# Queries projected once, convolution output in image order, and later places for layer 1's and layer 3's small steps

## The chip, the cores and the metric

The kernel runs on one core of a Trainium2 chip. Time is device time in microseconds (us), the median of the runs: 2678.51 us before the change (three runs, 2678.45 to 2680.86). TensorE (PE in the profile) multiplies matrices into PSUM; VectorE (DVE) and ScalarE (ACT) work element by element; GpSimd (POOL) and SyncE (SP) mostly start transfers.

## The reference

A batch of 4 images of 64 x 64 pixels and 64 channels, in float32, goes through four layers:

- layer 0: self-attention over the 4096 pixels of an image. With q, k, v of 64 channels, `energy = q @ k.T`, softmax over its last axis, and `out[n] = sum_m attn[m, n] * v[m]`; then `gamma * out + x`.
- layer 1: a convolution block. Layer norm over channels, a pointwise product to 256 channels, a depthwise 3 x 3 convolution, the product of the two halves of channels, a channel gate (`sca`: the mean over pixels through a 128 x 128 matrix), a pointwise product back to 64 channels, and a residual. Then a second layer norm, a pointwise product to 256 channels, the product of halves, a product back to 64, and a residual.
- layer 2: attention over "channels by height" as the reference's reshape has it: scores are `xf.T @ xf` with 4096 x 4096 entries, softmax, products, residual.
- layer 3: a non-local block with 32 inner channels (`theta`, `phi`, `g`), softmax over 4096 x 4096, a product back to 64 channels, batch norm over all images, and a residual.

So each image has three 4096 x 4096 score matrices, whose exponentials are never stored as a whole.

## The kernel before

**Layout.** `X` holds an image as 128 partitions by 2048: 64 channels for each of two halves `s` of the pixels. `tok(x, s, j)` is the piece of 512 pixels number `j` of half `s`. Scores, exponentials and products are cut into items: an item of layer 0 makes 16 score matmuls into four PSUM tiles of 1024 columns, ScalarE takes the exponentials, and 8 product matmuls of an earlier item accumulate in PSUM. An item of layer 2 is 16 scores and 16 products, an item of layer 3 is 8 and 4. The matmuls use TensorE as several small arrays: 64 x 64 for the scores of layers 0 and 2, 128 rows by 64 columns for layer 0's products, 32 x 64 and 128 x 32 in layer 3.

**PSUM and buffers.** `new_ps` rotates through three PSUM tiles of 1024 columns, for scores and everything else; `new_acc` through two of 512 columns, for the accumulated products and for the sums `z` of layer 3. `new_t` rotates through two scratch tiles of 1024 columns, `new_e` through six tiles of exponentials.

**The order of the work** on TensorE, ScalarE and VectorE is written out by hand; each of these engines works through its list in that order. The main list has the items of all layers. The other steps (projections, layer 1, transposes) are generators in two lanes, `conv` and `misc`. Each item has a nominal time (3.6 us in layer 0, 4.6 in layer 2, 1.0 in layer 3), which is added to the lanes' clock twice per item, once after the scores and once after the products. A lane's step is recorded when the clock has reached its due time, and the number that a step yields is added to that due time:

```python
self.next = max(self.next, self.now - 8.0) + next(self.gens[0])   # Lane.step
while self.gens and self.next <= self.now: self.step()            # Lane.tick
```

So a yield says how much nominal time lies between two steps. A step with a small yield can be recorded in the same half item as the one before it.

**Steps that the change and the prediction touch.**

- `project0` (L961) makes layer 0's queries and values of the next image during the items of the present one. The folded weight `wq` has the same 64 columns twice, so each of four matmul groups (L971) writes the same queries to partitions 0 to 63 and 64 to 127 of `m.q`; L975 adds the bias and L983 that of the values.
- `norm` (L1052): squares on ScalarE (L1056), column sums on TensorE (L1062), then square, difference, Ln and Exp on 512 columns (L1067 to L1070), eight transfers that spread the result over the partitions (L1074), and two products on VectorE (L1082).
- `layer1`: pointwise products (L1091) into the padded image `pad` (L1113), nine taps per quarter and half of the channels on VectorE (L1128, L1130), the gate (L1133), the channel gate (L1136 to L1143), `pw2` (L1148) and its sum (L1156). Taps and gate write `yg` in the order of image columns; the reading matmul L1148 picks alternate columns out of it. In the second part, L1166 and L1168 take the two pointwise halves, and L1172 multiplies their product `u`.
- `close2` (L1252) divides layer 2's products and adds the residual (L1259, L1261); `open3` (L1267) starts with layer 3's theta projection (L1278), which reads that sum.
- In layer 3, VectorE adds up the exponentials (L1346, L1348), `totals` closes the sums (L1362), copies `z` out of PSUM (L1370), inverts it by Ln and Exp on ScalarE (L1374, L1375) and VectorE steps (L1376 to L1378). For the last half of images 0 and 1 it stands directly before the first layer-2 products of another image, which take two accumulators.

Of the kernel before, what the change touches and what calls it, by code (L numbers as in the profile page):

```python
# [8 lines left out]
F32 = mybir.dt.float32  # L9
# [682 lines left out]
def fast_path(ctx: ExitStack, tc: tile.TileContext, a: dict, out: bass.AP, bad):  # L692
    nc = tc.nc
# [29 lines left out]
    def new_big(name):  # L723
        return big.tile([128, 4096], F32, tag="big", name=name)
# [236 lines left out]
    def project0(b):  # L961
        x, m = X[:, b], im[b]
        m.q, yv = new_big("q"), new_big("yv")
        m.y = yv[:, 0:2048]
        m.v = yv[:, 2048:4096].rearrange("p (t c) -> p t c", c=C)
        for j, w in ((0, "q"), (0, "v"), (1, "q"), (2, "q"), (1, "v"), (3, "q")):
            ps = new_ps()
            if w == "q":
                for o in range(0, 128, 64):
                    for s in range(2):  # L970
                        mm(  # L971
                            ps[o : o + 64, bass.ts(s, 512)], wq[64 * s : 64 * s + 64, o : o + 64],
                            tok(x, s, j), start=True, stop=True,
                        )
                nc.vector.tensor_scalar_add(  # L975
                    m.q[:, 0:N].rearrange("p (s n) -> p s n", s=2)[:, :, bass.ts(j, 512)],
                    ps.rearrange("p (s n) -> p s n", s=2), bqk,
                )
            else:
                for i in range(8):  # L980
                    mm(ps[:, bass.ts(i, 128)], x[:, bass.ts(8 * j + i, 128)], wv, start=True, stop=True)  # L981
                for s in range(2):
                    nc.vector.tensor_add(  # L983
                        m.v[:, 16 * s + 8 * j : 16 * s + 8 * j + 8, :],
                        ps.rearrange("p (t s c) -> p t s c", s=2, c=C)[:, :, s, :],
                        bv.unsqueeze(1).to_broadcast([128, 8, C]),
                    )
            yield 3.4
# [62 lines left out]
    def norm(x, y):  # L1051


        sq = [new_t("sq"), new_t("sq")]
        for i in range(2):
            act(sq[i], x[:, bass.ts(i, 1024)], AF.Square)  # L1056
        yield 4.0
        ps = new_ps()
        for i, src in enumerate(((x, x), (sq[0], sq[1]))):
            for j in range(4):  # L1060
                c = 512 * j if i == 0 else 512 * (j % 2)
                mm(  # L1062
                    ps[32 * j : 32 * j + 32, bass.ts(i, 512)], jsel, src[j // 2][:, c : c + 512],
                    start=True, stop=True,
                )
        t = new_t()
        act(t[:, 0:512], ps[:, 0:512], AF.Square)  # L1067
        stt(t[:, 0:512], t[:, 0:512], -1.0, ps[:, 512:1024], ALU.mult, ALU.add)
        act(t[:, 0:512], t[:, 0:512], AF.Ln, bias=eps1)
        act(t[:, 512:1024], t[:, 0:512], AF.Exp, scale=-0.5)  # L1070
        yield 7.0
        for j in range(4):
            for h in range(2):
                nc.sync.dma_start(  # L1074
                    out=y[64 * h : 64 * h + 64, bass.ts(j, 512)],
                    in_=t[32 * j + 16 * h : 32 * j + 16 * h + 16, 512:1024]
                    .unsqueeze(1).to_broadcast([16, 4, 512]),
                )
        yield 26.0
        for jp in range(2):  # L1080
            cols = bass.ts(jp, 1024)
            nc.vector.tensor_mul(y[:, cols], y[:, cols], x[:, cols])  # L1082
            yield 1.8

    def layer1(b):
# [10 lines left out]

        y = xn.tile([128, 2048], F32, tag="xn", name="xn")
        yield from norm(x, y)
        yg = new_big("yg")[:, 0:N].rearrange("p (w h) -> p w h", h=H)
        ysum = sm.tile([128, 4], F32, tag="ysum", name="ysum")  # L1100
        for r in (1, 0):
            pad = new_pad()
            nc.gpsimd.memset(pad[:, 0:PW], 0.0)
            nc.gpsimd.memset(pad[:, 65 * PW : 66 * PW + 2], 0.0)
            nc.gpsimd.memset(
                pad[:, PW : 65 * PW].rearrange("p (w h) -> p w h", h=PW)[:, :, 0:1], 0.0
            )
            inner = pad[:, PW + 1 : 65 * PW + 1].rearrange("c (p q s h) -> c q p s h", p=2, s=2, h=PW)
            for j in range(4):
                ps = new_ps()  # L1110
                pointwise(ps, pw1, r, y, j)
                for s in range(2):
                    act(  # L1113
                        inner[:, bass.ts(j, 4), :, s, 0:H],
                        ps[:, bass.ts(s, 512)].rearrange("c (q p h) -> c q p h", p=2, h=H),
                        AF.Identity, bias=pwb[:, 0, r : r + 1],
                    )
                yield 3.5
            for j in range(4):
                w0 = 16 * j  # L1120
                y2 = yg[:, w0 : w0 + 16, :]
                out_ = y2 if r else new_t("y1").rearrange("p (w h) -> p w h", h=H)
                for k in range(9):
                    o = (w0 + k % 3) * PW + k // 3
                    win = pad[:, o : o + 16 * PW].rearrange("p (w h) -> p w h", h=PW)[:, :, 0:H]
                    wt = V("L1_conv_dw_w", 2 * k + r)
                    if k == 0:
                        nc.vector.tensor_scalar(out_, win, wt, V("L1_conv_dw_b", r), ALU.mult, ALU.add)  # L1128
                    else:
                        stt(out_, win, wt, out_, ALU.mult, ALU.add)  # L1130
                    yield 1.8
                if not r:
                    stt(y2, out_, 1.0, y2, ALU.mult, ALU.mult, accum_out=ysum[:, j : j + 1])  # L1133
                    yield 1.8
        ytot = sm.tile([128, 1], F32, tag="ytot", name="ytot")
        nc.vector.tensor_reduce(ytot, ysum, AX.X, ALU.add)  # L1136
        yield 3.5
        ps = new_ps()
        mm(ps[:, 0:1], sca, ytot, start=True, stop=True)
        ch = sm.tile([128, 1], F32, tag="ch", name="ch")  # L1140
        nc.vector.tensor_scalar(ch, ps[:, 0:1], 1.0 / N, V("L1_conv_sca_b"), ALU.mult, ALU.add)
        pw2s = sm.tile([128, C], F32, tag="pw2s", name="pw2s", bufs=1)
        nc.vector.tensor_scalar_mul(pw2s, pw2, ch)  # L1143
        yield 3.5
        for j in range(4):
            ps = new_ps()
            for s in range(2):
                mm(  # L1148
                    ps[64 * s : 64 * s + 64, 0:512], pw2s,
                    yg.rearrange("c (p q s) h -> c q p s h", p=2, s=2)[:, bass.ts(j, 4), :, s, :],  # L1150
                    start=True, stop=True,
                )
            t = new_t()
            act(t[:, 0:512], ps[:, 0:512], AF.Identity, bias=resb[:, 0:1], scale=V("L1_conv_beta"))
            xs = x[:, bass.ts(j, 512)]
            nc.vector.tensor_add(xs, xs, t[:, 0:512])  # L1156
            yield 3.5
        z = xn.tile([128, 2048], F32, tag="xn", name="xn")
        yield from norm(x, z)
        for j in range(4):  # L1160
            t, u = new_t(), new_t("u")
            for r in range(2):
                ps = new_ps()
                pointwise(ps, pw3, r, z, j)
                if r == 0:
                    act(t, ps, AF.Identity, bias=pwb[:, 1, 0:1])  # L1166
                else:
                    stt(u, ps, pwb[:, 1, 1:2], t, ALU.add, ALU.mult)  # L1168
                yield 3.5
            ps = new_ps()  # L1170
            for s in range(2):
                mm(ps[64 * s : 64 * s + 64, 0:512], pw4, u[:, bass.ts(s, 512)], start=True, stop=True)  # L1172
            act(t[:, 0:512], ps[:, 0:512], AF.Identity, bias=resb[:, 1:2], scale=V("L1_conv_gamma"))
            xs = x[:, bass.ts(j, 512)]
            nc.vector.tensor_add(xs, xs, t[:, 0:512])
            yield 3.5
# [75 lines left out]
    def close2(b):  # L1252
        x, m = X[:, b], im[b]
        nc.vector.tensor_reduce(sums2[:, b, :], m.zs, AX.X, ALU.add)
        rz = sm.tile([128, 32], F32, tag="rz2", name="rz2")
        nc.vector.reciprocal(rz, sums2[:, b, :])
        for i in range(4):
            d = m.ph[:, bass.ts(i, 512)].rearrange("p (w h) -> p w h", h=H)
            nc.vector.tensor_mul(d, d, rz[:, bass.ts(i, 8)].unsqueeze(2).to_broadcast([128, 8, H]))  # L1259
            xs = x[:, bass.ts(i, 512)]  # L1260
            nc.vector.tensor_add(xs, xs, m.ph[:, bass.ts(i, 512)])  # L1261
            yield 2.0

# [46 lines left out]
    def layer3(b):  # L1312
# [53 lines left out]

        def totals(nb):
            sums()
            yz = st["yz"]
            nc.scalar.copy(yz[:, 512:1024], st["z"])  # L1370

            t = new_t("inv")
            r, d = t[:, 0:512], t[:, 512:1024]
            act(r, yz[:, 512:1024], AF.Ln)  # L1374
            act(r, r, AF.Exp, scale=-1.0)  # L1375
            nc.vector.tensor_mul(d, yz[:, 512:1024], r)  # L1376
            stt(d, d, -2.0, r, ALU.add, ALU.mult, accum_out=inv3[:, b, nb : nb + 1])
            stt(yz[:, 0:512], d, -1.0, yz[:, 0:512], ALU.mult, ALU.mult)  # L1378

# [224 lines left out]
```

## Time and profile before

| | us |
|---|---|
| span of the profiled execution | 2674.3 |
| TensorE busy | 2614.5 |
| ScalarE busy | 1722.9 |
| VectorE busy | 1349.0 |
| layer 0's scores and products (L1005, L1030) | 473.3 and 467.3 |
| layer 2's (L1208, L1225) | 472.4 and 467.9 |
| layer 3's (L1324, L1352) | 313.4 and 272.0 |
| queries (L971), all images | 17.0 |
| taps, other than first (L1130), both halves | 164.3 and 164.3 |

A group's line in the profile has the engine, the operation, the tiles it writes and reads, their shapes, the count, the busy time and the mean of one. A float32 matmul appears as two records, so x128 of L971 are 64 matmuls. A timeline row has start, duration, and in brackets the idle time of the engine just before it and what ended that. Layer 0 runs to about 1050 us with layer 1 beside it, layer 2 of images 0 and 1 to about 1580 with the rest of layer 1, and then layers 3 and 2 take turns.

### The profile page before, as it was taken

The page shows a single profiled execution, that of the slowest core. Times are in us where ns is not written, and L with a number is a line of the kernel's source. Part 1 is how long each engine was busy: PE and PEld are TensorE (multiplying, and loading weights), DVE is VectorE, ACT ScalarE, POOL GpSimd, SP SyncE. Part 2 cuts the span into 40 slices and gives each one's busy share as a digit, 9 for nine tenths or more (in the row PEclk, how much of TensorE's full clock was granted, in tenths as well). Part 3 has the DMA queues.
Part 4 walks back from the last instruction along what each step waited for, and adds up shares of the span by engine and source line. Part 5 has one row for each costly group of instructions (what it writes and reads, how often), then busy time and mean ns, then how long its engine had stood idle before and what let it go on. Part 6 is the DMA issues. An engine that isn't in the chain of part 4 may idle for free.

```text
span 2674.3 us, 50670 instructions
## 1 busy us (share of the span) xinstructions
PE 2614.5 (98%) x22393; PEld 831.3 (31%) x22393; DVE 1349.0 (50%) x1505; ACT 1722.9 (64%) x2796; POOL 16.4 (1%) x66
## 2 busy tenths in 40 slices
PE   8999999999999999999999999999999999999996
PEld 3333233323323333433333322243322333322222
DVE  3242387733777336641475148810068600098997
ACT  4545655555565665665656568856578756578886
POOL 2000000000000000000000000000000000000000
PEclk9999999999999999999999999999999999999998
DMA  3000000000000100010010100010000010010001
GB/s 73 1 1 1 16 1 1 1 17 17 1 1 1 33 16 1 1 32 1 17 33 1 33 1 1 2 33 1 17 2 1 5 29 1 1 33 1 1 2 65
DMA packets 22505, 33.30 MB, mean 12 GB/s; under 512 B 3484, under 2 KB 11909, under 8 KB 22277
## 3 DMA queue, kind: packets, MB, share of 16 engines
q1 hardware_dynamic: 21205, 28.87, 4.8%
q8 instruction: 177, 2.90, 0.5%
q0 software_dynamic: 672, 0.56, 0.1%
q10 hardware_dynamic: 400, 0.56, 0.1%
q14 instruction: 51, 0.42, 0.1%
HBM read 4.80 MB, written 4.19 MB: 3 GB/s over the span
## 4 chain that ended last, share of the span: by engine, by line
PE 92%; DVE 4%; ACT 2%; issue 1%; DMA 0%; ACTq 0%; DVEq 0%
PE acc L1030 17%; PE ps L1005 17%; PE acc L1225 16%; PE ps L1208 15%; PE ps L1324 10%; PE acc L1352 9%; PE ps L1091 2%; DVE yg L1130 1%; PE accz L1341 1%; DVE tg L1348 1%; ACT e L1216 1%; PE ps L981 1%; PE ps L1172 1%; PE ps L1148 1%; PE ps L1062 1%
## 5 line engine op out<-in xcount | busy, mean ns | idle before, releaser
L1010 ACT ACTIVATE e<-ps 128x1024 f32<-128x1024 f32 x512 | 516.6, 1024 | 336.4 <-PE ps L1005 217.7
L1216 ACT ACTIVATE e<-ps 128x1024 f32<-128x1024 f32 x512 | 516.6, 1024 | 317.4 <-PE ps L1208 317.2
L1330 ACT ACTIVATE e<-ps 128x1024 f32<-128x1024 f32 x512 | 495.4, 1022 | 87.3 <-PE ps L1324 78.9
L1348 DVE TENSOR_TENSOR tg<-tg,e 128x2048 f32<-128x2048 f32 x214 | 490.4, 2291 | 24.1 <-ACT e L1330 5.8
L1005 PE MATMUL ps<-X,q 64*64 64x512 f32 x4096 | 473.3, 596 | 8.4 <-ACT e L1010 4.4
L1208 PE MATMUL ps<-ko 64*64 64x512 f32 x4096 | 472.4, 593 | 5.4 <-ACT e L1216 2.4
L1225 PE MATMUL acc<-e,X 64*64 64x512 f32 x4096 | 467.9, 591 | 2.1 <-DVE X L1037 1.5
L1030 PE MATMUL acc<-e,vq 128*64 128x512 f32 x2048 | 467.3, 598 | 0.0
L1037 DVE SCALAR_TENSOR_TENSOR yv<-acc,gam,yv 128x512 f32<-128x512 f32 x224 | 168.0, 750 | 345.6 <-PE acc L1030 334.2
L1324 PE MATMUL ps<-tg,ph 32*64 32x512 f32 x4096 | 313.4, 613 | 0.5 <-ACT e L1330 0.5
L1352 PE MATMUL acc<-e,tg 128*32 128x512 f32 x2048 | 272.0, 603 | 1.5 <-ACT yz L1358 1.5
L1208 PEld LDWEIGHTS ps<-ko 64*64 64x64 f32 x4096 | 158.7, 133 | 291.6 <-issue 190.2
L1225 PEld LDWEIGHTS acc<-e,X 64*64 64x64 f32 x4096 | 164.1, 133 | 273.7 <-issue 255.3
L1005 PEld LDWEIGHTS ps<-X,q 64*64 64x64 f32 x4096 | 142.3, 132 | 322.7 <-issue 220.3
L1030 PEld LDWEIGHTS acc<-e,vq 128*64 128x64 f32 x2048 | 136.5, 136 | 315.8 <-issue 297.5
L1233 DVE TENSOR_TENSOR ph<-ph,acc 128x512 f32<-128x512 f32 x16 | 11.0, 687 | 383.4 <-ACT ph L1232 383.4
L1130 DVE SCALAR_TENSOR_TENSOR y<-pad,vec,y 128x1024 f32<-128x1024 f32 x128 | 164.3, 1284 | 6.3 <-ACT pad L1113 2.4
L1130 DVE SCALAR_TENSOR_TENSOR yg<-pad,vec,yg 128x1024 f32<-128x1024 f32 x128 | 164.3, 1283 | 3.7
L1324 PEld LDWEIGHTS ps<-tg,ph 32*64 32x64 f32 x4096 | 79.8, 129 | 221.2 <-issue 142.4
L1352 PEld LDWEIGHTS acc<-e,tg 128*32 128x32 f32 x2048 | 43.5, 108 | 202.3 <-issue 196.3
L1216 ACT ACTIVATION_READ_ACCUMULATOR e<-ps 128x1 f32 x512 | 106.3, 208 | 0.0
L1010 ACT ACTIVATION_READ_ACCUMULATOR e<-ps 128x1 f32 x512 | 106.2, 207 | 0.0
(179 smaller groups left out, 964.5 us busy)
## 6 DMA issues: line engine op xcount, KB each, us to landing
xn<-t SPq DMA_DIRECT2D x64, 128.0 KB
ph<-tg SPq DMA_DIRECT2D x64, 128.0 KB
ko<-ko SPq DMA_DIRECT2D x16, 256.0 KB
out_dram<-o SPq DMA_DIRECT2D x8, 512.0 KB
xr<-in_x_dram SPq DMA_DIRECT2D x14, 256.0 KB
xr<-in_x_dram ACTq DMA_DIRECT2D x2, 256.0 KB
pw<-in_L_conv_pw_w_dram POOLq DMA_DIRECT2D x4, 64.0 KB, 4.2
sca<-in_L_conv_sca_w_dram POOLq DMA_DIRECT2D x1, 64.0 KB, 5.7
```

Source lines behind the costliest of these rows:

```text
L1005: mm(ps[64 * c : 64 * c + 64, bass.ts(r, 512)], m.q[rows_, 128 * t + 64 * c : 128 * t + 64 * c + 64], x[rows_, bass.ts(g, 512)], start=Tru ...
L1010: act(es[g // 2][:, bass.ts(g % 2, 1024)], ps, AF.Exp, bias=SHIFT0, accum_out=zs[:, g : g + 1],)
L1030: mm(accs[g][64 * r : 64 * r + 64, :], vq, es[half][:, 1024 * g + 512 * r : 1024 * g + 512 * r + 512], start=t == 2 * p, stop=t == 2 * p + 1,)
L1037: stt((x if p == 15 else m.y)[:, cols], accs[g], gam0, (m.y if p else x)[:, cols], ALU.mult, ALU.add,)
L1130: stt(out_, win, wt, out_, ALU.mult, ALU.add)
L1208: mm(ps[64 * c : 64 * c + 64, bass.ts(r, 512)], m.ko[rows_, 128 * jb + 64 * c : 128 * jb + 64 * c + 64], m.ko[rows_, bass.ts(2 * ib + r, 5 ...
L1216: act(es[n, jb], ps, AF.Exp, bias=SHIFT2, accum_out=m.zs[:, jb, ib : ib + 1])
L1225: mm(acc[r][64 * c : 64 * c + 64, :], xw[rows_, jb, :], es[n, jb][rows_, bass.ts(c, 512)], start=jb == 0, stop=jb == 31,)
L1324: mm(tiles[kp][64 * c : 64 * c + 64, bass.ts(i, 512)], m.ph[rows_, 128 * mc + 64 * c : 128 * mc + 64 * c + 64], m.th[rows_, bass.ts(nb, 51 ...
L1330: act(e[:, bass.ts(kp, 1024)], tiles[kp], AF.Exp)
L1348: nc.vector.tensor_add(esum, esum, e)
L1352: mm(st["y"][32 * k : 32 * k + 32, :], m.gx[:, mc, :], e[:, bass.ts(k, 512)], start=mc == 0, stop=mc == 31,)
```

## The change

Five edits. For images 1 to 3, `project0` multiplies each half of the queries once, into the 64 partitions of one of its two places, and transfers bring them to the other 64; image 0 keeps the old way. The convolution writes `yg` in image order (the last tap of the first half of channels, and the gate, in two parts each), so that `pw2` reads it contiguously. Several yields in `norm` and `layer1` are moved or made larger, so that Ln and Exp, the channel gate and the last pointwise product are recorded later than what feeds them; the wait before the normalising products is made shorter. `close2` yields longer after its last sum, so that `open3` comes later. `totals` reads `z` from PSUM directly and no longer copies it.

```diff
-        for j, w in ((0, "q"), (0, "v"), (1, "q"), (2, "q"), (1, "v"), (3, "q")):
+        once = ((0, "once"), (0, "v"), (1, "once"), (1, "v"))
+        for j, w in once if b else ((0, "q"), (0, "v"), (1, "q"), (2, "q"), (1, "v"), (3, "q")):
             ps = new_ps()
-            if w == "q":
+            if w == "once":
+                for o in range(2):
+                    for s in range(2):
+                        mm(
+                            ps[64 * o : 64 * o + 64, bass.ts(s, 512)], wq[64 * s : 64 * s + 64, 0:64],
+                            tok(x, s, 2 * j + o), start=True, stop=True,
+                        )
+                qs = m.q.rearrange("p (s n) -> p s n", s=2)
+                for o in range(2):
+                    own, other = slice(64 * o, 64 * o + 64), slice(64 - 64 * o, 128 - 64 * o)
+                    n = bass.ts(2 * j + o, 512)
+                    nc.vector.tensor_scalar_add(
+                        qs[own, :, n], ps[own, :].rearrange("p (s n) -> p s n", s=2), bqk[own, :]
+                    )
+                    nc.sync.dma_start(out=qs[other, :, n], in_=qs[own, :, n])
+            elif w == "q":
...
         stt(t[:, 0:512], t[:, 0:512], -1.0, ps[:, 512:1024], ALU.mult, ALU.add)
+        yield 5.0
         act(t[:, 0:512], t[:, 0:512], AF.Ln, bias=eps1)
         act(t[:, 512:1024], t[:, 0:512], AF.Exp, scale=-0.5)
-        yield 7.0
+        yield 4.0
...
-        yield 26.0
+        yield 14.0
...
-        yg = new_big("yg")[:, 0:N].rearrange("p (w h) -> p w h", h=H)
-        ysum = sm.tile([128, 4], F32, tag="ysum", name="ysum")
+        yg = new_big("yg")
+        yw = yg.rearrange("c (s q p h) -> c p q s h", s=2, p=2, h=H)
+        ysum = sm.tile([128, 8], F32, tag="ysum", name="ysum")
...
+                    elif k < 8 or not r:
+                        stt(y1, win, wt, y1, ALU.mult, ALU.add)
                     else:
-                        stt(out_, win, wt, out_, ALU.mult, ALU.add)
+                        for s in range(2):
+                            stt(
+                                yw[:, j // 2, bass.ts(j % 2, 8), s, :], win[:, s:16:2, :], wt,
+                                y1[:, s:16:2, :], ALU.mult, ALU.add,
+                            )
                     yield 1.8
                 if not r:
-                    stt(y2, out_, 1.0, y2, ALU.mult, ALU.mult, accum_out=ysum[:, j : j + 1])
+                    for s in range(2):
+                        y2 = yw[:, j // 2, bass.ts(j % 2, 8), s, :]
+                        stt(
+                            y2, y1[:, s:16:2, :], 1.0, y2, ALU.mult, ALU.mult,
+                            accum_out=ysum[:, 2 * j + s : 2 * j + s + 1],
+                        )
...
         nc.vector.tensor_reduce(ytot, ysum, AX.X, ALU.add)
-        yield 3.5
+        yield 5.0
...
         nc.vector.tensor_scalar_mul(pw2s, pw2, ch)
-        yield 3.5
+        yield 5.0
...
-                    ps[64 * s : 64 * s + 64, 0:512], pw2s,
-                    yg.rearrange("c (p q s) h -> c q p s h", p=2, s=2)[:, bass.ts(j, 4), :, s, :],
+                    ps[64 * s : 64 * s + 64, 0:512], pw2s, yg[:, bass.ts(4 * s + j, 512)],
...
                     stt(u, ps, pwb[:, 1, 1:2], t, ALU.add, ALU.mult)
-                yield 3.5
+                yield 5.0 if r else 3.5
...
             nc.vector.tensor_add(xs, xs, m.ph[:, bass.ts(i, 512)])
-            yield 2.0
+            yield 2.0 if i < 3 else 6.0
...
-            yz = st["yz"]
-            nc.scalar.copy(yz[:, 512:1024], st["z"])
+            yz, z = st["yz"], st["z"]
...
-            act(r, yz[:, 512:1024], AF.Ln)
+            act(r, z, AF.Ln)
             act(r, r, AF.Exp, scale=-1.0)
-            nc.vector.tensor_mul(d, yz[:, 512:1024], r)
+            nc.vector.tensor_mul(d, z, r)
```

More of the change, by code (lines that the diff above doesn't have):

```diff
@@ L1120, in layer1 @@
                 w0 = 16 * j
-                y2 = yg[:, w0 : w0 + 16, :]
-                out_ = y2 if r else new_t("y1").rearrange("p (w h) -> p w h", h=H)
+                y1 = new_t("y1").rearrange("p (w h) -> p w h", h=H)
                 for k in range(9):
@@ L1127, in layer1 @@
                     if k == 0:
-                        nc.vector.tensor_scalar(out_, win, wt, V("L1_conv_dw_b", r), ALU.mult, ALU.add)
-                    else:
-                        stt(out_, win, wt, out_, ALU.mult, ALU.add)
+                        nc.vector.tensor_scalar(y1, win, wt, V("L1_conv_dw_b", r), ALU.mult, ALU.add)
+                    elif k < 8 or not r:
+                        stt(y1, win, wt, y1, ALU.mult, ALU.add)
+                    else:
+                        for s in range(2):
[3 more added lines that the diff above has]
+                            )
                     yield 1.8
                 if not r:
-                    stt(y2, out_, 1.0, y2, ALU.mult, ALU.mult, accum_out=ysum[:, j : j + 1])
+                    for s in range(2):
[4 more added lines that the diff above has]
+                        )
                     yield 1.8
```

## The prediction

> **What bounds the kernel now.** I read the page's busy shares and chain first, then TensorE's waits, then the timeline around each wait.
>
> ```profile
> PE 2614.5 (98%) x22393; PEld 831.3 (31%) x22393; DVE 1349.0 (50%) x1505; ACT 1722.9 (64%) x2796; POOL 16.4 (1%) x66
> ...
> PE 92%; DVE 4%; ACT 2%; issue 1%; DMA 0%; ACTq 0%; DVEq 0%
> ```
>
> TensorE is busy for 2614.5 of 2674.3 us and carries 92% of the chain. So two things shorten this kernel: fewer matmuls, and fewer of the 59.8 idle us. TensorE's timeline puts about 11 us of idle time in the first 15 us and about 21 after 2600 us; the change touches neither. Some 29 us lie between, and the waits name them:
>
> ```profile
> PE ps L1172 <- DVE u L1168: 5.0, 3, 1.8
> PE ps L1005 <- ACT e L1010: 4.4, 5, 1.2
> PE ps L1278 <- DVE X L1261: 4.1, 3, 2.8
> PE ps L1005 <- DVE q L975: 3.3, 4, 1.4
> PE ps L1208 <- ACT e L1216: 2.4, 2, 1.2
> ```
>
> Each is a matmul recorded too soon behind the ScalarE or VectorE work that feeds it or frees its PSUM tile. The columns are total, times, longest.
>
> **What the Trainium skill says.** "TensorEngine Tiling (Array Packing)", Key Properties: changing the tiling mode drains the array, tiles of one mode run in parallel. The trace agrees: 16 score matmuls (32 records) take 3.43 us where layer 2 uses 64x64 tiles throughout, and 3.59 in layer 0, which alternates with 128x64. "Perfetto Trace Analysis", Optimization Strategy: on the engine that matters, find the gaps and make what they wait for start sooner; that is how I count below. "VectorE: DVE Perf Modes", the TRN2 errata section: a fixed cost per instruction, so halves cost more than the whole. The trace agrees (692 ns for 512 elements, 1219 for 1024).
>
> **The change part by part.**
>
> *Queries once, images 1 to 3.* Four q groups of four matmuls become two, so six groups go in all. One inserted group moves the next start by 0.91 to 0.97 us (L971 at 395.95, next at 396.86; 653.30, next at 654.26). At 0.94: −5.6 us. VectorE's work stays: one 128-partition add of 1.28 us becomes two of 64 partitions; a 64-partition copy of the same 1024 elements takes 1.215 (L1190), so I take 1.28 each. The copies to the other 64 partitions are DMAs of 256 KB; they have over ten items of 7.2 us before layer 0 of that image reads them, so they cost nothing. But a query group's PSUM tile is now held for 2.56 us, and only three such tiles exist. The place to look is image 2, whose projection falls among layer 1's taps:
>
> ```profile
> 397.28 2.60 DVE L1130 SCALAR_TENSOR_TENSOR yg<-pad,vec,yg 128x1024 f32<-128x1024 f32 x2
> 399.80 1.28 DVE L975 TENSOR_SCALAR q<-ps,bqk 128x1024 f32<-128x1024 f32 x1
> ```
> ```profile
> 399.18 1.09 PE L1005 MATMUL ps<-X,q 64*64 64x512 f32 x8 [0.42 <-ACT e L1010]
> 401.13 1.09 PE L1005 MATMUL ps<-X,q 64*64 64x512 f32 x8 [0.86 <-DVE q L975]
> ```
>
> The add queues behind two taps, and scores wait for its tile: that item's 16 matmuls took 5.18 us (396.86 to 402.04) instead of 3.49, a later one 4.11: 2.3 us lost now. In the changed program's recorded order, VectorE has T4, two q adds, two v adds, the layer-0 pair, its scale, a tap and a split tap, then two q adds. From the same start (391.8): 2.56 + 1.4 gives 395.7, pair and scale 397.9, taps 2.7 give 400.6, adds end at 403.2; the third score tile wants that PSUM at 396.86 + 1.8 = 398.7. Loss 4.5. Image 1: the first v add ends at 5.3 us where its tile is wanted at 4.8: 0.6. Image 3, with pads beside it: 0.8 by the same count. Together +5.9 −2.3 = +3.6.
>
> *Ln and Exp later.* Now ScalarE does Square, waits for VectorE, then Ln and Exp, while four score exponentials stand behind:
>
> ```profile
> 287.11 0.60 ACT L1067 ACTIVATE t<-ps 128x512 f32<-128x512 f32 x1 [2.05 <-PE ps L1062]
> 288.52 0.72 ACT L1069 ACTIVATE t<-t,eps 128x512 f32<-128x512 f32 x1 [0.81 <-DVE t L1068]
> 289.28 0.63 ACT L1070 ACTIVATE t<-t 128x512 f32<-128x512 f32 x1
> 289.81 1.00 ACT L1010 ACTIVATE e<-ps 128x1024 f32<-128x1024 f32 x1
> ```
> ```profile
> 290.96 1.09 PE L1005 MATMUL ps<-X,q 64*64 64x512 f32 x8 [1.24 <-ACT e L1010]
> ```
>
> The fourth tile of scores waits 1.24 us. The same gap of 1.18 stands at 539.5, 883.4, 1194.5 and 1273.9: 6.0 us. A lane steps at most once per 3.6 (layer 0) or 4.6 (layer 2) nominal us, so a yield of 5.0 always puts half an item, 3.4 us or more of TensorE, in between. In the new order every Ln has exponentials or such a half item ahead of it. −6.0. The DMA behind Exp lands within 8 us of it (Exp ended near 1272.8, second product at 1280.8); the first product now comes 18 nominal us after Exp, so the shorter yield costs nothing.
>
> *Pointwise products and the sca steps later*, by the same 5.0: the three waits of L1172 (1.58, 1.84, 1.55), L1139 (0.98), L1148 (0.69): −6.6. *Projections later* (6.0 after the last sum): 2.79 + 0.98 + 0.28: −4.0.
>
> *A side effect of moved steps.* In image 2's second norm the new order records the squares and their sums in one step, right behind 16 scores. ScalarE ends its exponentials some 1.6 us after those scores, then two squares of 1.07: the second half of the sums can start 3.7 us after the scores instead of 0.9: +2.8. ScalarE has nothing urgent behind it. Elsewhere the squares keep a half item of room. Layer 2's transposes (waits of 0.66, 0.42, 0.87, 0.47 now) get new neighbours: −1.0, with 0 to −1.5 as bounds.
>
> *Image order.* Eight taps or gates per image become two of half size: 0.16 us more each for a tap (2 x 0.72 against 1.284), 0.24 for a gate with its accumulator: 1.6 us of VectorE per image. Beside layer 0, nine taps and their share of layer-0 work take 15.73 us in 16.16, ten steps with a gate 17.55 in 17.95; with the additions 15.9 and 17.8. It fits, barely, so 0. TensorE's pw2 matmuls read contiguously instead of in runs of 64; L1148 costs 16.8 us as L1172 costs 17.1 with contiguous reads, so nothing is gained.
>
> *No copy of z.* ScalarE saves 0.60 seven times. Inside layer 3 it is nearly full, and after each of five totals the scores stretch (2.07 against 1.11 us); they shorten by the copy: −3.1. At the two turns from layer 3 to layer 2 the copy was what freed the accumulator:
>
> ```profile
> 1728.33 0.60 ACT L1358 COPY yz<-acc 128x512 f32<-128x512 f32 x1
> 1728.79 0.62 ACT L1370 COPY yz<-accz 128x512 f32<-128x512 f32 x1
> 1729.45 0.63 ACT L1374 ACTIVATE inv<-yz 128x512 f32<-128x512 f32 x1
> 1730.11 0.63 ACT L1375 ACTIVATE inv<-inv 128x512 f32<-128x512 f32 x1
> ```
>
> The new products need z's buffer; the old copy released it at 1729.4. Now the VectorE product after Exp releases it: 1728.8 + 0.63 + 0.66 + 0.7 = 1730.9, 1.45 later; behind that matmul stand all of TensorE's scores. Twice: +2.9.
>
> Sum: −5.6 + 3.6 − 6.0 − 6.6 − 4.0 + 2.8 − 1.0 − 3.1 + 2.9 = −17.0. From 2678.5: **2661.5 us**.
>
> **The rivals.** *No new waits*: VectorE runs ahead more than counted, and the 5.9, 2.8 and 2.9 do not appear: 2678.5 − 28.6 = 2650. For it: most VectorE idle time lies just before those points. Against: the query wait is there already, with half the hold time. *New waits take half*: all three query projections lose 4.5 as image 2 does (+7.6), and another sum or transpose loses 2: 2671. For it: three PSUM tiles are few wherever lanes meet. Against: images 1 and 3 project without taps beside them. *VectorE becomes the bound beside layer 0*: if half a tap with strided rows costs as much as a whole one, eight times 1.28 us per image meet a slack of 0.4: 0.88 x 8 x 3 = 21 us: 2682, slower than before. For it: VectorE is 93% busy there already. Against: 512-element rows of every kind take 0.69 to 0.75.
>
> **How the numbers follow.** The counted sum 0.60; no new waits 0.15; half 0.18; VectorE bound 0.07. The range of 2652 to 2671 covers the counted case with its unknowns (transposes 1.5, query waits ±4, totals ±3) and most of the two neighbours. Faster by over 0.2% means under 2673.2: 0.60 + 0.15 + 0.12 = 0.87; within 0.2%: 0.07; slower 0.06.
>
> **What would show it.** TensorE's waits on u, on Exp-delayed e, on ytot and on the last sum of close2 gone; a wait of some 4 us on the query add near 390 to 410 us; one wait of 2 to 3 us of the sums of squares on sq in layer 2; products of layer 2 waiting over 1 us on VectorE's inv twice; scores after totals at 1.45 us rather than 2.07. I am wrong if VectorE's layer-0 pair makes TensorE's L1030 matmuls wait during taps, or if the query copies' DMAs are waited for.

## The result and the profile after

The changed kernel takes 2656.11 us (median of four, 2655.98 to 2657.46) against 2679.69 of the kernel before beside it: a ratio of 0.9912, 95% interval 0.9895 to 0.9929. That is 23.6 us less, where 17.0 were predicted; 2656.1 lies inside the range of 2652 to 2671, 5.4 us under the forecast.

The same two lines of the page, the busy shares and the chain:

```profile
PE 2606.3 (98%) x22345; PEld 824.7 (31%) x22345; DVE 1352.9 (51%) x1553; ACT 1718.8 (65%) x2789; POOL 16.4 (1%) x66
...
PE 94%; DVE 3%; ACT 2%; issue 1%; DMA 0%; ACTq 0%; DVEq 0%
```

TensorE has 48 fewer records and 8.2 us less work, VectorE 48 more instructions and 3.9 us more, ScalarE 7 fewer and 4.1 us less (seven copies of z at 0.60). TensorE's share of the chain rises from 92% to 94%: waits went.

TensorE's waits in the same view (total, times, longest), leaving out the start and the end, which hardly changed:

```profile
PE ps L1021 <- DVE q L980: 4.1, 2, 3.1
...
PE acc L1252 <- DVE inv L1402: 1.6, 2, 0.8
PE ps L1078 <- ACT sq L1072: 1.6, 1, 1.6
PE ps L1235 <- ACT ko L1217: 1.6, 3, 0.7
```

Of the five waits shown of the kernel before, only that on the query add is still high in the list, and it has grown. The waits on u, on ytot and on layer 2's last sum (X) are gone, of those of scores on e two of 0.4 us are left in layers 0 and 2. What stands there now are the three waits that the prediction named: the query add, the squares, and VectorE's inv at the turns.

Idle time isn't all that a wait costs, so below I also use the *shift*: the start of each group of score or product matmuls in one trace, less the start of the same group in another. It is flat while both kernels do the same, and steps where one loses time. Taken from 62.6 us (after the constants are set up) to the last group of layer 3, the kernel before is 23.2 us behind the changed one, like the timed 23.6. The spans of the two pages differ by only 20.0, because from 47 to 54 us the changed kernel's trace has a stretch in which TensorE was granted half its clock, 3.1 us of start that the other trace doesn't have.

| stretch of the changed kernel | counted in the prediction | shift |
|---|---|---|
| 63 to 276 us: image 1's queries | −1.3 | −1.2 |
| 276 to 789: two norms, two query projections, sca of image 0 | −3.9 | −4.5 |
| 789 to 1044: one norm, transposes | −1.5 | −0.6 |
| 1044 to 1552: layer 2 of images 0 and 1 | −9.3 | −15.3 |
| 1552 to 2563: layer 3, two turns, last projection | −1.2 | −1.6 |

The transposes' −1.0 is divided by their waits. So the surplus of 6 us lies in one stretch, layer 2 of images 0 and 1 with layer 1 of images 2 and 3 beside it.

**The new waits, one by one.** First TensorE, then VectorE, in the timeline of the changed kernel, where image 2's queries are projected (start, duration, instruction, idle time before it):

```profile
403.63 1.09 PE L1021 MATMUL ps<-X,q 64*64 64x512 f32 x8 [3.14 <-DVE q L980]
```
```profile
399.65 1.41 DVE L1150 SCALAR_TENSOR_TENSOR yg<-pad,vec,y 128x512 f32<-128x512 f32 x2
400.98 2.59 DVE L980 TENSOR_SCALAR q<-ps,bqk 64x1024 f32<-64x1024 f32 x2
```

The two adds queue behind a tap and a split tap and end at 403.57; the scores start at 403.63. Those sixteen score matmuls took 7.46 us (397.08 to 404.54) in place of 3.49: 3.97 lost, 4.5 predicted. Image 1 waits 0.2, image 3 1.0. A half tap takes 0.75 us (counted 0.72), an add of 64 partitions 1.28 (counted 1.28).

ScalarE in the first norm of layer 1, where the Ln stood ahead of four score exponentials:

```profile
289.92 1.02 ACT L1026 ACTIVATE e<-ps 128x1024 f32<-128x1024 f32 x1 [0.36 <-PE ps L1021]
...
293.92 0.74 ACT L1086 ACTIVATE t<-t,eps 128x512 f32<-128x512 f32 x1
```

Now four exponentials run first, and TensorE's 32 score records go through in 3.67 us with no gap.

The sums of squares in image 2's second norm, TensorE's timeline:

```profile
1154.86 1.06 PE L1078 MATMUL ps<-X,jsel 128*32 128x512 f32 x8
1157.54 2.00 PE L1078 MATMUL ps<-sq,jsel 128*32 128x512 f32 x8 [1.62 <-ACT sq L1072]
1159.47 1.95 PE L1252 MATMUL acc<-e,X 64*64 64x512 f32 x16
```

4.61 us from the first to the third line, 1.86 without a wait: 2.75 lost, 2.8 predicted; the idle time is only 1.62. At the two turns the product behind Ln and Exp waits 0.81 us on VectorE's inv, and the shift steps by 1.39 each (1.45 predicted). After each of five totals it falls by 0.65, 3.25 in all (3.1 predicted).

### The profile page after: what moved, and what is told of

Read it like the earlier page. It is cut to its first block, busy times and chain, and to the rows that moved or that the text cites. A ratio compares the mean times of both kernels' runs of the same rounds, so it can differ in the third digit from the quotient of the medians.

```text
span 2654.3 us, 50638 instructions
## 1 busy us (share of the span) xinstructions
PE 2606.3 (98%) x22345; PEld 824.7 (31%) x22345; DVE 1352.9 (51%) x1553; ACT 1718.8 (65%) x2789; POOL 16.4 (1%) x66
## 4 chain that ended last, share of the span: by engine, by line
PE 94%; DVE 3%; ACT 2%; issue 1%; DMA 0%; ACTq 0%; DVEq 0%
PE acc L1046 17%; PE acc L1252 17%; PE ps L1021 17%; PE ps L1235 16%; PE ps L1351 11%; PE acc L1379 9%; PE ps L1108 2%; PE accz L1368 1%; ACT e L1243 1%; PE ps L1199 1%; PE ps L1176 1%; PE ps L1078 1%; PE ps L1330 1%; DVE tg L1375 1%; PE ps L997 0%
## 5 line engine op out<-in xcount | busy, mean ns | idle before, releaser
L1046 PE MATMUL acc<-e,vq 128*64 128x512 f32 x2048 | 467.5, 599 | 0.0
L1147 DVE SCALAR_TENSOR_TENSOR y<-pad,vec,y 128x1024 f32<-128x1024 f32 x240 | 308.1, 1284 | 8.1 <-ACT pad L1131 1.0
L1046 PEld LDWEIGHTS acc<-e,vq 128*64 128x64 f32 x2048 | 136.2, 137 | 314.9 <-issue 294.2
L1131 ACT ACTIVATE pad<-ps,pwb 128x512 f32<-128x512 f32 x64 | 44.6, 697 | 44.2 <-PE ps L1108 37.8
```

Of the source, the lines that this page charges most:

```text
L1046: mm(accs[g][64 * r : 64 * r + 64, :], vq, es[half][:, 1024 * g + 512 * r : 1024 * g + 512 * r + 512], start=t == 2 * p, stop=t == 2 * p + 1,)
L1147: stt(y1, win, wt, y1, ALU.mult, ALU.add)
```

## Experiments

Each run is the changed kernel with the edit shown. *Shift* is measured in the traces against the changed kernel, from 62.6 us to the last group; it repeats to some 0.1 us where nothing differs, while the timed medians scatter by about 2 us. Each shift comes from one trace, and it includes any stretch at half the clock that this execution had (last section). A *room* is the number that a step yields: the nominal time up to its lane's next step.

| run | timed, us (range) | ratio to before (95%) | shift |
|---|---|---|---|
| u_query | 2657.02 (2654.92–2657.98) | 0.9920 (0.9907–0.9934) | +2.25 |
| u_norm | 2675.74 (2673.12–2677.78) | 0.9989 (0.9982–0.9995) | +22.24 |
| u_layer1 | 2659.55 (2659.08–2661.13) | 0.9930 (0.9917–0.9944) | +4.55 |
| u_close2 | 2660.41 (2657.53–2662.65) | 0.9931 (0.9918–0.9945) | +6.60 |
| u_image | 2655.67 (2654.03–2657.07) | 0.9916 (0.9902–0.9929) | −0.22 |
| u_z | 2657.67 (2654.59–2659.22) | 0.9920 (0.9907–0.9934) | +2.85 |
| z_turn | 2652.38 (2650.84–2657.92) | 0.9909 (0.9895–0.9922) | −2.86 |
| q_early | 2653.50 (2650.90–2653.78) | 0.9908 (0.9893–0.9923) | −2.33 |
| sq_later | 2665.94 (2664.27–2666.41) | 0.9949 (0.9936–0.9963) | +9.48 |
| best | 2657.54 (2657.43–2659.69) | 0.9922 (0.9909–0.9936) | +3.52 |
| late | 2666.25 (2664.70–2673.15) | 0.9960 (0.9947–0.9974) | +11.84 |
| best2 | 2648.27 (2648.22–2650.48) | 0.9886 (0.9871–0.9901) | −4.75 |

**Queries as before**

```diff
-        for j, w in once if b else (...):
+        for j, w in once if False else (...):
```


> The changed kernel with the old query projection in all four images (four groups per image, both heads of a pair at once); everything else stays changed. My theory (the queries are worth what the prediction counted: six groups of 0.94 us, less the new waits for their PSUM tile, 3.97 + 0.23 + 0.99 us measured, plus the 2.3 us of old waits that come back): about 2 us slower than the changed kernel, 2658. Rival (the 6 us by which the result beats the prediction lie in the queries): 6 to 9 us slower than the changed kernel, 2662 to 2665.

+2.25 us by the shift, near the −5.6 + 3.6 of the prediction, and not the place of the surplus. (By the timed medians it is 0.9, and the ranges overlap; both are far from the rival's 6 to 9.)

**Ln and Exp as before**

```diff
-        yield 5.0
         act(... AF.Ln ...); act(... AF.Exp ...)
-        yield 4.0
+        yield 7.0
         (broadcast DMAs)
-        yield 14.0
+        yield 26.0
```


> The changed kernel with layer 1's Ln and Exp recorded as before: behind the copy of the sums in the same step, and the longer room behind them. Theory S (a removed wait is worth the time from start to start of the matmuls around it): five waits come back at 1.47 us each, 7.3 us slower than the changed kernel, 2663.4; or 4.6 slower if the shifted steps also take away image 2's wait of the sums for the squares (2.75 us). Theory G (worth the visible gap only): 6.0 slower, 2662.1, or 3.3 slower.

Neither theory: 22.2 us, as if nearly the whole gain hung on these three numbers. But the edit does two things. It puts Ln and Exp ahead of the exponentials, and it makes each norm 10 nominal us longer, so all that follows in layer 1 comes later. The run *late* keeps the second and leaves out the first.

**The room behind the DMAs longer, and nothing else**

```diff
-        yield 14.0
+        yield 24.0
```


> The changed kernel with one number altered: the room between the broadcast DMAs behind Exp and layer 1's first product at 24.0 in place of 14.0, which gives each norm the same whole length (37.0) as in the run that recorded Ln and Exp as before. Ln and Exp stay where the change put them, so none of the removed waits is put back; only the layer 1 lane comes later beside the other lanes. Theory P (what is left of the gain beyond the removed waits is the position of the lane: in the run with Ln and Exp as before it met layer 2's key copies and the squares at the wrong time): 10 to 16 us slower than the changed kernel, 2666 to 2672. Theory W (the waits of Ln and Exp are worth it all; the prediction held that this room costs nothing): within 2 us of the changed kernel.

Theory P: +11.8 by the shift, all of it in layer 2's stretch (+11.75 from 1044 to 1552 us). TensorE and VectorE of this run where layer 2's keys of image 1 are transposed:

```profile
1167.41 3.12 PE L1235 MATMUL ps<-ko 64*64 64x512 f32 x16 [4.51 <-ACT ko L1217]
```
```profile
1161.27 3.92 DVE L1147 SCALAR_TENSOR_TENSOR y<-pad,vec,y 128x1024 f32<-128x1024 f32 x3
1165.10 1.21 DVE L1217 COPY ko<-ps 64x1024 f32<-64x1024 f32 x1
```

Layer 1's taps, which in the changed kernel are done by then, now stand ahead of the key copy on VectorE; ScalarE's half of the copy (L1217, at 1166.35) waits 5.72 us for VectorE's, and the next scores wait 4.51 us for the PSUM tile that both read. (In the changed kernel that wait is 0.67.) Image 3's transposes meet the next norm in the same way (1.33 and 1.75 us in place of 0.47). One first product of layer 1's second part waits 2.59 us and starts at 1233.00. The profile names no releaser, but VectorE's timeline shows one: the normalising product that it reads stands behind the addition of layer 2's products (1231.07), and its first half ends at 1232.90. With 0.25 more at the squares these are 9.3 us; the rest is in two half-clock stretches (below).

The two runs then differ only in where Ln and Exp stand, and with them the transfers behind (2 nominal us). From *late* to *u_norm* the shift steps six times at such a wait, by 1.47, 1.69, 1.41, 1.41, 1.41 and 1.41: 8.8 us for gaps that show 1.24, 1.33 and four times 1.18, 7.3 in all. The other 1.6 us between the two runs are a half-clock stretch of u_norm at 404 us. The first of them in TensorE's timeline of u_norm:

```profile
291.26 1.09 PE L1021 MATMUL ps<-X,q 64*64 64x512 f32 x8 [1.24 <-ACT e L1026]
```

So a wait is worth its start-to-start cost, 0.23 to 0.36 us more than the idle time here, and theory S has the size of the single wait right. What it had no term for was the position of everything behind it.

**Layer 1's other rooms as before**

```diff
-        yield 5.0   (sca, pw2s)          /  yield 5.0 if r else 3.5   (pointwise)
+        yield 3.5                        /  yield 3.5
```


> The changed kernel with the room ahead of the sca steps, the second pointwise product and the pointwise products of layer 1 back at 3.5 from 5.0. Theory S: the five waits (on u three times, on ysum and ytot) come back at what they cost from start to start, with the stretched scores behind one of them: 9.1 us slower than the changed kernel, 2665.2. Theory G (visible gaps alone): 6.6 slower, 2662.7.

+4.55, below both theories, and not for the reason of either. With the short norms kept, layer 1 runs some 27 us earlier at its end, and its steps have other neighbours: only one of the three u waits returns (1.56 at 1445), ytot twice at 0.3; the wait on the squares vanishes; and image 3's query wait grows from 0.99 to 2.23, with a half-clock stretch behind it. The sum of waits of the kernel before can't be had back by undoing one part.

**Layer 3's projections as before**

```diff
-            yield 2.0 if i < 3 else 6.0
+            yield 2.0
```


> The changed kernel with layer 3's projections recorded 2.0 behind layer 2's last sum, as before, in place of 6.0. Theory S: start to start the first projection's wait cost 4.9 us, with the two others 6.0 us in all: 6.0 slower than the changed kernel, 2662.1. Theory G (visible gaps 2.79, 0.98 and 0.28): 4.05 slower, 2660.2.

Of the 6.60, 2.5 come from a half-clock stretch at 400 to 407 us, before this code runs; 4.1 are left: 3.0 at the first projection, 1.1 at the last. That is theory G's number, by another route. In the kernel before, taps of layer 1 stood between the four sums on VectorE and the projection waited 2.79 once; here the taps have moved away, and it waits four times 0.23 to 0.28, each at some 0.5 us more from start to start.

**Output in the old order**

```diff
-   8 half taps and 8 half gates into yw[:, :, :, s, :], pw2 from yg[:, bass.ts(4 * s + j, 512)]
+   4 taps and 4 gates of 1024, pw2 from the strided view of yg
```


> The changed kernel with layer 1's convolution output in the old order: whole taps and gates of 1024 elements, the second pointwise product reading runs of 64. Theory: within 0.5 us of the changed kernel, 2656.1, since VectorE's 1.6 us per image and TensorE's reads both bear on nothing. Rival A (contiguous reads help TensorE): 2 us or more slower than the changed kernel. Rival B (VectorE is the bound beside the taps): 2 us or more faster.

−0.22: neither VectorE's additions nor TensorE's contiguous reads bear on the time, as predicted.

**z copied always, and z copied at the turns**

```diff
+            nc.scalar.copy(yz[:, 512:1024], z)     # u_z: always; z_turn: only if nb == 1 and b < 2
+            z = yz[:, 512:1024]
```


> The changed kernel with z copied out of its accumulator in every total of layer 3, as before. Theory: five totals inside the stage lose 0.65 us each (3.25), the two turns from layer 3 to layer 2 gain 1.34 each (2.7), and the last image's end loses nothing that can be seen: 0.6 us slower than the changed kernel, 2656.7. Rival (the copy costs its 0.60 us in all seven totals and nothing comes back at the turns): 4.2 slower, 2660.3.

> The changed kernel with z copied out only in the two totals that end layer 3 of images 0 and 1, where the next layer 2 product waits for z's buffer. Theory: the products start 1.34 us earlier twice: 2.7 us faster than the changed kernel, 2653.4. Rival (the scores queued behind take the time back, since ScalarE has the copy to do as well): same as the changed kernel, 2656.1.

u_z: 0.65 more at each of five totals, 1.4 less at each turn: 0.4 net (0.6 expected); the other 2.45 of its shift are again the stretch at 404 us. z_turn: −2.86, the two turns alone, and the wait on inv is gone. Both terms of the prediction were real and almost cancelled; keeping the copy in two totals of seven takes the one without the other.

**Image 2's projection earlier**

```diff
-            misc_from[32 * b + 16] = gens + [project0(b + 1)]
+            misc_from[32 * b + (3 if b == 1 else 16)] = gens + [project0(b + 1)]
```


> The changed kernel with image 2's layer 0 projection taken up from the third item of image 1's stage on, beside the norms, not from the sixteenth, beside the taps. Theory: the query add no longer queues behind two taps, and the 3.97 us that the scores of image 2's projection lose fall to under 1: 3 to 3.5 us faster than the changed kernel, 2653. Rival (the wait comes from holding one of three PSUM tiles for two adds, wherever the projection stands): within 1 us of the changed kernel.

−2.33, between the two. TensorE's wait beside the norm, where no tap stands ahead of the adds:

```profile
300.57 1.95 PE L1021 MATMUL ps<-X,q 64*64 64x512 f32 x16 [1.27 <-DVE q L980]
```

So of the 3.97 lost at image 2, some 2.5 were the queue behind the taps, and 1.5 are left where no tap stands ahead, by the hold of one of three PSUM tiles for two adds (2.59 us). That rest depends on the place too: image 1's projection, with the same hold, waits 0.2.

**Sums of squares later**

```diff
             act(sq[i], x[:, bass.ts(i, 1024)], AF.Square)
-        yield 4.0
+        yield 5.0
```


> The changed kernel with the sums of squares of every layer 1 norm recorded 5.0 behind their squares in place of 4.0, so that half an item always lies between. Theory: image 2's second norm no longer waits for its squares, 2.75 us faster than the changed kernel, 2653.4. Rival (the later steps move another wait into place, or the second half of the sums was hidden): within 1 us of the changed kernel.

The wait on the squares went, and the shift fell by 3.6 there, but the run is 9.5 us slower: every norm is 1.0 longer, and three waits appear elsewhere, of 1.97 (a pad at 742 us), 2.13 (the turn from layer 0 to layer 2) and 2.80. The last one, VectorE and then TensorE:

```profile
1332.68 0.69 DVE L1288 TENSOR_TENSOR X<-X,ph 128x512 f32<-128x512 f32 x1
1333.29 2.60 DVE L1147 SCALAR_TENSOR_TENSOR y<-pad,vec,y 128x1024 f32<-128x1024 f32 x2
1335.81 0.69 DVE L1286 TENSOR_TENSOR ph<-ph,rz 128x512 f32<-128x512 f32 x1
```
```profile
1337.27 1.82 PE L1305 MATMUL ps<-X,thw 64*32 64x512 f32 x4 [2.80 <-DVE X L1288]
```

Two taps have come to stand between layer 2's sums, and the projection of layer 3 waits as it did in the kernel before. Each of the three waits has a half-clock stretch behind it.

**The repairs together**

> The three repairs together: z copied at the two turns, image 2's projection beside the norms, the sums of squares 5.0 behind their squares. Theory (each wait stands alone on TensorE's path, so the gains add): 2.7 + 3.5 + 2.75 = 9 us faster than the changed kernel, 2647. Rival (the shifted lanes meet other waits): 3 to 5 us faster, 2651 to 2653.

> The two repairs that gained, together, without the later sums of squares: z copied at the two turns and image 2's projection beside the norms. Theory (they lie in different stages, and add): 2.86 + 2.3 = 5.2 us faster than the changed kernel, 2651. Rival (the later start of image 2's lane gives part of it back at the turns): 2.5 to 3.5 us faster, 2653.

With the later sums of squares (*best*) +3.5: the loss of that edit outweighs the two repairs. Without it (*best2*: z_turn and q_early) −4.75 of −5.19: the two lie in different stages and nearly add. Its ratio to the kernel before, 0.9886, is the lowest of all; its interval and the changed kernel's still overlap, but all four of its times (up to 2650.48) lie under all four of the changed kernel's (from 2655.98), with 2678.77 and 2679.69 for the kernel before beside them.

## Why the prediction was right, and where its size was off

*Right in direction and in most terms.* Queries: −5.6 + 3.6 = −2.0, undoing them cost 2.25, and image 2's wait came at the place named (3.97 against 4.5). Squares: 2.75 against 2.8. Totals: 3.25 against 3.1; turns 1.39 against 1.45 each. Image order: 0.2 against 0. VectorE did not become the bound: a half tap takes 0.75 us, layer 0's products (L1046) wait for nothing beside the taps, and undoing the order gained nothing; so that rival falls. New waits did appear, so the one without them falls too, although its 2650 is about as far from the result as the 2661.5. The one in which all three images lose 4.5 falls as well: images 1 and 3 wait 0.2 and 1.0.

*The term that was mis-sized: the removed waits.* The prediction summed the idle gaps of TensorE (−6.0, −6.6, −4.0). The traces show more in the stretch from 1044 to 1552 us, 15.3 against 9.3, and from the trace of the kernel before the 6.0 can be put down to four things. A removed wait saves the time from start to start, 0.1 to 0.25 us above the gap for each of the six on u, ytot and e there (about 1.1), and at the first projection of layer 3 some 4.9 (1331.80 to 1338.64, less 1.9 for those matmuls) where 3.07 of idle time shows (1.8). One of the u waits, 1.84 us at 1508.8, was followed by a half-clock stretch in which 32 score records took 5.36 us (1.85). And the turn from layer 0 to layer 2, where a product waited 1.54 us on X before, waits 0.35 now, which was not counted (1.2). Together 5.95; small waits on pads (1.1 in all) went as well, and one of 0.4 on ph came. These are TensorE's lines of the kernel before at the turn, at the first projection, and behind the u wait at 1508.8:

```profile
1052.85 3.89 PE L1225 MATMUL acc<-e,X 64*64 64x512 f32 x29 [1.54 <-DVE X L1037]
1337.66 1.05 PE L1278 MATMUL ps<-X,thw 64*32 64x512 f32 x4 [2.79 <-DVE X L1261]
1509.83 5.36 PE L1208 MATMUL ps<-ko 64*64 64x512 f32 x32
```

The size of the single wait is tested by late against u_norm; this division of the rest is read from the traces, not tested.

*The step that was wrong.* "[T]he first product now comes 18 nominal us after Exp, so the shorter yield costs nothing" treats the room as a cost of its own place only. Lengthening it by 10, with nothing else altered, cost 11.8 us. A room sets when all later steps of layer 1 are recorded, and so which of VectorE's taps stand ahead of layer 2's key copies, of its last sums and of the turns. The change shortened the norms (37 to 27 nominal us) while it lengthened the other rooms, and layer 1 of the last image ended at 1496 us instead of 1546. Of these places its taps met only the turn from layer 0, for 0.35 us. The prediction did not work out that the positions would fall well; that they did was luck. It checked the new order at the places it knew of, and for the rest assumed that positions cost nothing. Undoing one part shifts them again, which is why the parts undone (2.25, 22.24, 4.55, 4.1, 0.4, −0.2; the 4.1 and 0.4 without the half-clock stretch at 404 us) add to 33 and not to 23.

## What to carry over

A room in a hand-recorded order is a position for everything behind it: price an edit by what the *whole* lane then stands beside on the in-order engines, and confirm it by altering the room alone, with the operation left in place. Count a wait from start to start of the matmuls around it, not by the idle time shown. And where an edit helps in one place and hurts in another (z copied in five totals, missed at two turns), make it at the places where it helps.

## What was not expected of the hardware

After some TensorE gaps the granted clock halves for 3.4 or 6.8 us. Between 404 and 409 us the changed kernel and u_z do the same work after the same gap of 3.14 us. The windows (length, busy time and instructions by engine, granted clock, DMA share, GB/s) of the changed kernel and of u_z:

```profile
403.60:406.10 2.50, 2.47 (x21) 1.11 (x22) 0.00 (x0) 1.31 (x3) 0.00 (x0) 1.00 0.97 200
```
```profile
404.20:406.70 2.50, 2.45 (x12) 0.79 (x16) 0.00 (x0) 0.40 (x1) 0.00 (x0) 0.50 0.96 200
```

The clock column reads 0.50 in place of 1.00, 12 matmul records fall into 2.5 us where 21 did, and u_z loses 2.45 us for a cause that its edit has nothing to do with. In the fourteen traces, between 100 and 2590 us, there are 24 gaps of 1.8 us or more; behind 15 of them matmul records lasted 1.1 us instead of 0.59. There are 14 gaps of 1.4 to 1.8 us, and none of them was followed by such a stretch. The losses read from the shifts are 1.6 to 2.5 us each. So in these traces a gap of over about 1.8 us can cost nearly twice what it shows, and does so in one execution and not in the next.

The clock records of the traces show in the main what decides it. In each trace, all changes of the clock lie whole steps of 3.41 us apart. Between 100 and 2590 us, each of the fifteen half-clock stretches begins right behind a step in which TensorE was idle for 1.84 us or more. Of all steps at full clock with that much idle time, only three (1.85, 1.94 and 2.02 us) were followed by full clock. So what counts is not the whole gap, but how much of it falls into one step. The kernel before and sq_later have the same gap ahead of a projection of layer 3, 2.79 and 2.80 us. These are two steps of each, the kernel before first:

```profile
1332.80:1336.20 3.40, 1.78 (x10) 0.14 (x4) 3.33 (x5) 0.00 (x0) 0.00 (x0) 1.00 0.00 0
1336.20:1339.60 3.40, 1.94 (x16) 0.55 (x20) 2.21 (x4) 0.00 (x0) 0.00 (x0) 1.00 0.00 0
```
```profile
1334.00:1337.40 3.40, 0.60 (x6) 0.13 (x4) 3.33 (x5) 0.00 (x0) 0.00 (x0) 1.00 0.00 0
1337.40:1340.80 3.40, 3.40 (x15) 0.58 (x17) 2.43 (x3) 1.38 (x2) 0.39 (x3) 0.50 0.00 0
```

In the kernel before, the gap is split: with a wait of 0.28 just ahead of it, 1.6 us lie in the first step and 1.5 in the second, and the clock stays at 1.00. In sq_later all 2.80 us lie in one step, and the next runs at 0.50. Where the steps lie beside the program differs from one execution to the next, so an edit can't aim at them. This is read from fourteen traces; no run was made to test it, and between 1.84 and 2.02 us the idle time alone doesn't decide.
